# A graph layer over sorted edges: one scheduling context, a longer tail of single steps, and early VectorE operations with one SBUF input

## The chip, the core and the metric

The kernel runs on one NeuronCore of a Trainium2 chip. The core has TensorE (matrix products into PSUM; in profiles PE, its weight loads PEld), VectorE (DVE), ScalarE (ACT), GpSimd (POOL) and SyncE (SP), which run their own instruction queues in order and wait for each other through semaphores. Data come from HBM by DMAs, which SP, ACT and POOL issue. The metric is the device time of one execution in microseconds, as the median of several runs.

## The reference

The layer passes messages along 212,500 edges between 12,500 nodes of 64 features, and the edges are sorted by their destination `dst`:

```
h    = relu(concat(x[src], x[dst], edge_attr) @ mW1 + mb1)      # 212500 x 128
agg  = segment_sum(h @ mW2 + mb2, dst, 12500)                   # 12500 x 64
u    = relu(concat(x, agg) @ uW1 + ub1) @ uW2 + ub2
out  = layernorm(x + u)                                         # per node, no scale or shift
```

All is float32: x is 12500 x 64, edge_attr 212500 x 32, mW1 160 x 128, mW2 128 x 64, uW1 128 x 128, uW2 128 x 64.

## The kernel before

**Two programs.** `ordered` (from L96) relies on the order of the edges: the 384 edges of a group must have their destinations in a window of W = 32 nodes. It also counts on the chip whether that holds, and writes the answer to the one-element tensor `flag`. `unordered` (from L524) is a general program for any edge list. `gnn_layer` (L789) runs `ordered` in one scheduling context of the framework (`TileContext`), which ends with semaphore waits and barriers of all engines, then opens a second context. There every engine loads the flag (`values_load`, L796) and branches (`tc.If`, L798): `unordered` runs only if the flag is 0. With these inputs it is skipped.

**Work in groups.** G = 554 groups of 384 edges (3 tiles of 128; the last group has 148 edges) go through three parts. Each group also needs its rows x[src], which POOL fetches with one indirect DMA per tile (`gather`, L132, 1661 in all), up to AHEAD = 16 groups ahead, into a ring of 20 buffers `own.s`. VectorE writes the one-hot of the destinations within the window beside them (`onehot`, L303).

- `turn` (L309): TensorE transposes the three tiles (L315) into PSUM bank 0 of a buffer; ACT copies the result to `own.st` (L323), beside the edge attributes that SP loads (L263), and sums each row of it, which counts the edges per destination.
- `hidden` (L331): TensorE multiplies by the first layer's weights (L336), where the one-hot rows pick the window's part of x @ mW1 + mb1 from `own.wm`; ACT applies relu (L346, or L348 for the last group) into `own.h`.
- `sums` (L356): TensorE turns the counts into a row (L360) and multiplies relu's result by the one-hot (L362), which sums the messages per destination; VectorE adds both to `agg` (L371) and to row 0 of `xc` (L372).

Every four groups `windows` (L285) computes the next four `own.wm` (PE L289, VectorE copies L294), from columns of `xc` which `places` picks (L282). The second layer's weights are applied after the sum.

**Updates.** `plan` cuts the nodes into 25 chunks of 512 (the last has 212) and says after which group a chunk is closed: chunk 23 after group 546, the last one after all groups. `update` (L378) has four stages: `load` (xin, L384), `first` (PE L389 and L390, ACT L392, VectorE L393), `second` (PE L402, VectorE L404 to L409, ACT square root `rstd` L411) and `third` (VectorE L416, L419, output DMA on SP L423). `step_update` runs one stage each time `sums` is emitted.

**The order of the work** is written by hand: within `manual_schedule` every engine gets its instructions in the order in which they are emitted. `step` (L443) puts up to three parts together. Its first matmul waits for all that the parts need, and only the last matmul of the step counts on the semaphore, so whoever follows waits for the whole step. Steps take the two PSUM buffers `own.ps` in turn. The main loop (L488) at group k runs one step of turn k, hidden k-2 and sums k-4. From k = 548 on (SHORT = 6) `go_on(k, k - 1)` first catches up, in steps that pair one hidden with one sums, and then a step holds turn k alone.

**The front.** While the first gathers are issued, VectorE converts the groups' first destinations (`first_f`, L190, in SBUF), computes each edge's place in its window (`dlc`, 128 x 1662, L201 and L202) and counts the valid ones. For the count, L233 multiplies (place - 31) by place, and L234 compares that with 0 and accumulates:

```
    nc.vector.scalar_tensor_tensor(off, dlc, 1.0 - W, dlc, op0=ALU.add, op1=ALU.mult)
    nc.vector.tensor_scalar(off, off, 0.0, 0.0, ALU.is_le, ALU.add, accum_out=valid)
```

Of the kernel before, what the change touches and what calls it, by code (L numbers as in the profile page):

```python
# [19 lines left out]
P = 128  # L20
# [23 lines left out]
NEAR_GROUPS = 24  # L44
SHORT = 6
TIMES = 4
# [49 lines left out]
def ordered(ctx: ExitStack, tc: tile.TileContext, a, own, ok):  # L96
# [91 lines left out]

    first_f = temp.tile([P, G], F32, name="first_f")
    nc.vector.tensor_copy(first_f, first_i)  # L190
# [38 lines left out]


    off = temp.tile([P, G * TG], F32, name="off")
    valid = temp.tile([P, 1], F32, name="valid")
    nc.vector.scalar_tensor_tensor(off, dlc, 1.0 - W, dlc, op0=ALU.add, op1=ALU.mult)  # L233
    nc.vector.tensor_scalar(off, off, 0.0, 0.0, ALU.is_le, ALU.add, accum_out=valid)  # L234
    low = temp.tile([1, G], F32, name="low")
# [9 lines left out]
    vps = ups.tile([H, CH], F32, name="u_ps")  # L245
    nc.tensor.matmul(vps[0:1, 0:1], ones[:, 0:1], valid, start=True, stop=True)
    nv = temp.tile([1, 1], F32, name="nv")
    nc.vector.tensor_tensor(nv, vps[0:1, 0:1], nwrong, ALU.subtract)
    nc.vector.tensor_scalar(ok, nv, float(E), None, ALU.is_equal)

# [188 lines left out]

    users = [[], []]  # L440
    number = 0

    def step(gt=None, gh=None, gs=None):  # L443


        nonlocal number
        ps, used = own.ps[number % 2], users[number % 2]
        parts = [part(g, ps) for part, g in ((turn, gt), (hidden, gh), (sums, gs))
                 if g is not None]
        did = [i for part in parts for i in part[0]]  # L450
        after(did[0], *used, *(i for part in parts for i in part[1]))
        copies = None
        if gs is not None:
            for b in [b for b in xws if (b - 1) * SB <= gs][:1]:
                last, copies = windows(b, ps[:, 2, (TIMES + 1) * W : (TIMES + 1) * W + H])
                after(last, *used)
                did.append(last)
        for i in did[:-1]:
            tc.no_tile_sem_insts.add(i.ins.name)
            tc.add_to_no_dep_group("quiet", i.ins)  # L460
        used = []
        for n, (_, _, follow) in enumerate(parts):
            if gs is not None and n == len(parts) - 1:
                step_update(gs)
            used += follow(did[-1])
        if copies:
            copies()
            used += [wm_by[b * SB + i] for i in range(min(SB, G - b * SB))]
        users[number % 2] = used
        number += 1  # L470

# [5 lines left out]
    made = summed = 0  # L477

    def go_on(hidden_to, sums_to):

        nonlocal made, summed
        while made < hidden_to or summed < sums_to:
            gh = made if made < hidden_to else None
            gs = summed if summed < sums_to else None
            made, summed = made + (gh is not None), summed + (gs is not None)
            step(None, gh, gs)

    for k in range(G):  # L488
        if k < BITS:
            bit(k)  # L490
        if k % SB == 2:
            inputs(k // SB + 2)
        if k % SB == 1:
            places(k // SB + 1)
        onehot(k + 1)
        if k < G - SHORT:
            made, summed = max(0, k - 1), max(0, k - 3)
            step(k, k - 2 if k > 1 else None, k - 4 if k > 3 else None)
        else:
            go_on(k, k - 1)  # L500
            step(k)
        if k + AHEAD < G:
            gather(k + AHEAD)
    go_on(G, G)
    while now or waiting:
# [6 lines left out]
TAIL = E - FULL * R * P  # L512
LOAD = 8
NEAR = 3
# [9 lines left out]
def unordered(ctx: ExitStack, tc: tile.TileContext, a):  # L524
# [73 lines left out]
    with tc.tile_pool(name="nodes", bufs=3) as np_, tc.tile_pool(  # L598
        name="znodes_ps", bufs=2, space=PSUM
    ) as nps:  # L600
        for base, p, n in CHUNKS:
            s = np_.tile([P, R, H], F32, name="za")
            d = np_.tile([P, R, H], F32, name="zb")
            ps = nps.tile([P, R, 2, H], F32, name="zps")
            for k in range(n):
                nc.tensor.matmul(
                    ps[:p, k].rearrange("p s h -> p (s h)"), xT_sb[:, base + k : base + p * n : n],
                    w1ab.rearrange("k s h -> k (s h)"), start=True, stop=True,
                )
            nc.vector.tensor_copy(s[:p, :n], ps[:p, :n, 0, :])  # L610
            nc.scalar.activation(d[:p, :n], ps[:p, :n, 1, :], AF.Copy)
            rows = slice(base, base + p * n)
            nc.sync.dma_start(by_src[rows, :].rearrange("(p n) h -> p n h", p=p), s[:p, :n])
            nc.scalar.dma_start(by_dst[rows, :].rearrange("(p n) h -> p n h", p=p), d[:p, :n])
# [4 lines left out]
    with tc.tile_pool(name="zef", bufs=3) as efp, tc.tile_pool(  # L619
# [31 lines left out]
        def edges(g):  # L651
            m, p = tiles(g)
            t0 = g * R
            row = eps_.tile([P, R, P], F32, name="row")
            same = ep.tile([P, R, P], F32, name="same")
# [25 lines left out]

            hp = eps_.tile([P, R, H], F32, name="hp")
            t = ef_tiles[g // LOAD]
# [9 lines left out]

            sp = eps_.tile([P, R, H], F32, name="sp")
            for j in range(m):
# [20 lines left out]
    with tc.tile_pool(name="zupd", bufs=2) as up, tc.tile_pool(  # L716
        name="zupd_in", bufs=2
    ) as ip, tc.tile_pool(name="zupd_ps", bufs=2, space=PSUM) as ups, tc.tile_pool(
        name="zupd_ps1", bufs=1, space=PSUM
    ) as ups1:  # L720
        for base, p, n in CHUNKS:
# [14 lines left out]

            hT_ps = ups.tile([H, P * R], F32, name="hT_ps")
            cT_ps = ups1.tile([1, P * R], F32, name="cT_ps")
            for k in range(n):
# [7 lines left out]

            ag_ps = ups1.tile([D, P * R], F32, name="ag_ps")
            nc.tensor.matmul(ag_ps[:, :q], w2, hT[:, :q], start=True, stop=False)
# [5 lines left out]
            for k in range(n):  # L755
                nc.vector.tensor_copy(xk[:, k * p : (k + 1) * p],
                                      xT_sb[:D, base + k : base + q : n])
            u_ps = ups.tile([H, P * R], F32, name="zu_ps")
            nc.tensor.matmul(u_ps[:, :q], u1[:, 0, :], xk[:, :q], start=True, stop=False)
# [3 lines left out]

            o_ps = ups.tile([P, R, D], F32, name="o_ps")
            for k in range(n):
# [22 lines left out]

def gnn_layer(nc, a):  # L789
    with nc.sbuf_tensor("flag", [1, 1], I32) as flag:  # L790
        with ExitStack() as ctx:
            own = Own(nc, ctx)
            with tile.TileContext(nc) as tc, tc.manual_schedule():
                ordered(tc, a, own, flag.ap())
        with tile.TileContext(nc) as tc:
            good = nc.values_load(flag.ap()[0:1, 0:1], min_val=0, max_val=1,  # L796
                                  skip_runtime_bounds_check_because="a comparison's result")
            with tc.If(good == 0):  # L798
                with tc.manual_schedule():
                    unordered(tc, a)  # L800

# [33 lines left out]
```

## Time and profile before

| what | value |
|---|---|
| time, median of 3 runs | 2115.33 us (2114.32 to 2117.07) |
| the profiled execution's own time | 2125.18 us |
| its span, first to last instruction | 2123.5 us |
| busy: POOL / PE / PEld / DVE / ACT | 1578.7 / 1419.4 / 1207.0 / 574.6 / 554.4 us |
| gathers on POOL | 1661, 0.95 us each |
| mean granted TensorE clock | 0.931 |
| HBM read / written | 90.58 MB / 3.20 MB |

The profiled execution is 0.5% above the median of the runs. A line of the timeline has the start in us, the length in us, the engine, the source line, the operation, what it writes and reads, the number of merged instructions, and in brackets the idle time before it and what ended that. A "q" behind an engine's name is its instruction queue. A waits line says which operation waited for which, then the total in us, how many times, and the longest. A line of stretches has, for each engine, its busy time and its instruction count in brackets, then the granted TensorE clock as a share of full speed.

### The profile page before, as it was taken

The page shows a single profiled execution, that of the slowest core. Times are in us where ns is not written, and L with a number is a line of the kernel's source. Part 1 is how long each engine was busy: PE and PEld are TensorE (multiplying, and loading weights), DVE is VectorE, ACT ScalarE, POOL GpSimd, SP SyncE. Part 2 cuts the span into 40 slices and gives each one's busy share as a digit, 9 for nine tenths or more (in the row PEclk, how much of TensorE's full clock was granted, in tenths as well). Part 3 has the DMA queues.
Part 4 walks back from the last instruction along what each step waited for, and adds up shares of the span by engine and source line. Part 5 has one row for each costly group of instructions (what it writes and reads, how often), then busy time and mean ns, then how long its engine had stood idle before and what let it go on. Part 6 is the DMA issues. An engine that isn't in the chain of part 4 may idle for free. (4 is left out here: it accounts for less than half of the span.)

```text
span 2123.5 us, 30687 instructions
## 1 busy us (share of the span) xinstructions
PE 1419.4 (67%) x9439; PEld 1207.0 (57%) x9439; DVE 574.6 (27%) x3190; ACT 554.4 (26%) x1715; POOL 1578.7 (74%) x1668
## 2 busy tenths in 40 slices
PE   2766676676766667667666667676665766666766
PEld 2655565565555556556555556555554655555654
DVE  5222322223222222222223222222222222222222
ACT  1322222222222222222222222222222222222221
POOL 7777777777777777777777777777777777777772
PEclk9999989989999999999999898999999899999996
DMA  4321121122221212121212121221211121212110
GB/s 108 83 47 41 44 43 42 43 44 44 44 44 41 47 38 47 40 44 43 44 41 47 38 47 40 45 47 40 45 43 42 43 44 41 47 40 45 43 42 15
DMA packets 73364, 96.05 MB, mean 45 GB/s; under 512 B 33451, under 2 KB 40842, under 8 KB 73194
## 3 DMA queue, kind: packets, MB, share of 16 engines
q0 software_dynamic: 53152, 54.51, 13.5%
q1 hardware_dynamic: 19128, 39.03, 6.6%
q8 instruction: 80, 1.31, 0.3%
q14 instruction: 90, 0.74, 0.1%
q10 hardware_dynamic: 914, 0.46, 0.1%
HBM read 90.58 MB, written 3.20 MB: 44 GB/s over the span
## 5 line engine op out<-in xcount | busy, mean ns | idle before, releaser
L132 POOL DMA_INDIRECT own_s<-in_x,src_sb x1661 | 1577.9, 950 | 507.5 <-issue 354.3
L315 PE MATMUL own_ps<-own_ident,own_s 128*96 128x128 f32 x1661 | 300.5, 293 | 649.1 <-DVE own_s L303 233.2
L323 ACT ACTIVATE own_st<-own_ps 96x384 f32<-96x384 f32 x554 | 269.2, 486 | 1433.8 <-PE own_ps L362 1029.0
L315 PEld LDWEIGHTS own_ps<-own_ident,own_s 128*96 128x96 f32 x1661 | 172.8, 135 | 746.7 <-ACT own_h L346 671.7
L362 PE MATMUL own_ps<-own_s,own_h 128*128 128x128 f32 x3322 | 569.7, 313 | 0.0
L336 PE MATMUL own_ps<-own_wm,own_st 128*128 128x128 f32 x3322 | 502.1, 291 | 6.1 <-ACT own_st L323 5.4
L371 DVE TENSOR_TENSOR agg<-own_ps,agg 128x32 f32 x554 | 106.5, 192 | 1411.3 <-ACT own_h L346 1388.2
L362 PEld LDWEIGHTS own_ps<-own_s,own_h 128*128 128x128 f32 x3322 | 456.5, 208 | 24.2 <-issue 0.2
L336 PEld LDWEIGHTS own_ps<-own_wm,own_st 128*128 128x128 f32 x3322 | 454.8, 207 | 8.5 <-ACT own_st L323 7.7
L346 ACT ACTIVATE own_h<-own_ps 128x384 f32<-128x384 f32 x553 | 262.8, 475 | 17.6 <-issue 12.9
L294 DVE COPY own_wm<-own_ps 32x128 f32<-32x128 f32 x550 | 155.1, 282 | 6.2 <-issue 0.4
L303 DVE TENSOR_TENSOR own_s<-iota,dlc 128x96 f32<-128x96 f32 x554 | 133.2, 241 | 5.2 <-issue 1.1
L323 ACT ACTIVATION_READ_ACCUMULATOR own_st<-own_ps 96x1 f32 x554 | 105.4, 190 | 0.0
L360 PE MATMUL own_ps<-own_ident,own_counts 32*1 32x32 f32 x554 | 103.8, 187 | 1.1 <-ACT own_h L348 0.6
L372 DVE TENSOR_TENSOR xc<-own_ps,xc 1x32 f32 x554 | 99.2, 179 | 14.1 <-PE u_ps L390 13.5
L360 PEld LDWEIGHTS own_ps<-own_ident,own_counts 32*1 32x1 f32 x554 | 41.1, 74 | 74.1 <-issue 14.1
L282 DVE COPY xw<-xc 66x32 f32 x554 | 61.8, 173 | 2.9 <-DMA xc<-in_xT 2.3
L289 PE MATMUL own_ps<-w1b,xw 66*128 66x128 f32 (+1 forms) x276 | 56.8, 289 | 0.0
L402 PE MATMUL u_ps<-u,u 128*128 128x64 f32 (+1 forms) x196 | 48.5, 391 | 0.5 <-ACT u L392 0.5
L402 PEld LDWEIGHTS u_ps<-u,u 128*128 128x128 f32 (+1 forms) x196 | 47.5, 326 | 1.3 <-ACT u L392 1.1
L289 PEld LDWEIGHTS own_ps<-w1b,xw 66*128 66x128 f32 (+1 forms) x276 | 45.5, 207 | 0.1
L404 DVE TENSOR_TENSOR y<-u_ps,xin 128x256 f32<-128x256 f32 (+1 forms) x25 | 10.5, 419 | 81.9 <-PE u_ps L402 81.9
(57 smaller groups left out, 209.0 us busy)
## 6 DMA issues: line engine op xcount, KB each, us to landing
own_s<-in_x,src_sb POOLq DMA_INDIRECT x1661, 2.4
own_st<-in_efT SPq DMA_DIRECT2D x138, 192.0 KB, 2.8
xin<-in_x SPq DMA_DIRECT2D x24, 128.0 KB, 2.7
out<-o SPq DMA_DIRECT2D x24, 128.0 KB, 2.4
xc<-in_xT SPq DMA_DIRECT2D x12, 179.2 KB, 4.1
dlc_i<-in_dst_cols SPq DMA_DIRECT2D x1, 831.0 KB
xc<-in_xT SPq DMA_DIRECT2D x4, 179.5 KB, 4.3
src_sb<-in_src SPq DMA_DIRECT2D x13, 50.5 KB, 3.6
```

Of the source, the lines that this page charges most:

```text
L132: nc.gpsimd.indirect_dma_start(out=s[:p, j, W:], out_offset=None, in_=x[:, :], in_offset=bass.IndirectOffsetOnAxis(ap=src_sb[:p, g * TG + ...
L289: did = nc.tensor.matmul(wp[: n * W, :], xw[:, :n, :], w1b, start=True, stop=True)
L294: c = nc.vector.tensor_copy(wm[g % NW][:W, :], wp[i * W : (i + 1) * W, :])
L303: places_by[g] = nc.vector.tensor_tensor(own.s[g % RING][:, :, :W], iota.unsqueeze(1).to_broadcast([P, TG, W]), dlc[:, g * TG : (g + 1) * ...
L315: nc.tensor.transpose(xt[:, j * P : j * P + p], s[:p, j, :], ident[:p, :p])
L323: nc.scalar.activation(t[: D + W, c : c + n], xt[:, :n], AF.Copy, accum_out=counts[:, g : g + 1]), step)
L336: nc.tensor.matmul(pre[:p, j, :], t[:, c + j * P : c + j * P + p], wm[g % NW], start=True, stop=True)
L346: relu_by[g] = [nc.scalar.activation(h, pre, AF.Relu)]
L360: did = [nc.tensor.transpose(sg[0:1, TIMES, :], counts[:W, g : g + 1], ident[:W, :W])]
L362: did.append(nc.tensor.matmul(sg[:, :TIMES, :], h[:p, j, :], s[:p, j, :W].unsqueeze(1).to_broadcast([p, TIMES, W]), start=j == 0, stop=j = ...
L371: after(nc.vector.tensor_tensor(agg[:, at], sg[:, 0, :], agg[:, at], ALU.add), step),
L372: after(nc.vector.tensor_tensor(xc[0:1, at], sg[0:1, TIMES, :], xc[0:1, at], ALU.add), step),
```

## The change

- `gnn_layer` opens one context. The flag is a tile of that context, and the load and the branch follow `ordered` in it. The buffers of `Own` now stay allocated beside `unordered`, so that program gets fewer PSUM buffers, shared tags and LOAD = 4; it is still skipped.
- SHORT is 10. From k = 544 on every part is a step of its own with its own count on the semaphore: turn k, then up to two sums, then up to two hidden. `go_on` is gone; after the loop the remaining sums follow.
- `step` takes a list of (part, group). A part uses PSUM buffer g % 2 of its group, and the users of a buffer are kept per part.
- `first_f` lies in the PSUM buffer `own.ps[0]` instead of SBUF. The count of valid places is two comparisons, place >= 0 and place <= 31, each with one input and an accumulator; two matmuls add the two counts, and the constant they are compared with grows by the number of all places.

```
-SHORT = 6
+SHORT = 10
...
-    first_f = temp.tile([P, G], F32, name="first_f")
+    first_f = own.ps[0].rearrange("p a b -> p (a b)")[:, :G]
     nc.vector.tensor_copy(first_f, first_i)
...
     off = temp.tile([P, G * TG], F32, name="off")
-    valid = temp.tile([P, 1], F32, name="valid")
-    nc.vector.scalar_tensor_tensor(off, dlc, 1.0 - W, dlc, op0=ALU.add, op1=ALU.mult)
-    nc.vector.tensor_scalar(off, off, 0.0, 0.0, ALU.is_le, ALU.add, accum_out=valid)
+    valid = temp.tile([P, 2], F32, name="valid")
+    nc.vector.tensor_scalar(off, dlc, 0.0, 0.0, ALU.is_ge, ALU.add, accum_out=valid[:, 0:1])
+    nc.vector.tensor_scalar(off, dlc, W - 1.0, 0.0, ALU.is_le, ALU.add, accum_out=valid[:, 1:2])
...
-    nc.tensor.matmul(vps[0:1, 0:1], ones[:, 0:1], valid, start=True, stop=True)
+    for i in range(2):
+        nc.tensor.matmul(vps[0:1, 0:1], ones[:, 0:1], valid[:, i : i + 1], start=i == 0,
+                         stop=i == 1)
...
-    nc.vector.tensor_scalar(ok, nv, float(E), None, ALU.is_equal)
+    nc.vector.tensor_scalar(ok, nv, float(E + P * G * TG), None, ALU.is_equal)
...
-    users = [[], []]
-    number = 0
-    def step(gt=None, gh=None, gs=None):
-        nonlocal number
-        ps, used = own.ps[number % 2], users[number % 2]
-        parts = [part(g, ps) for part, g in ((turn, gt), (hidden, gh), (sums, gs))
-                 if g is not None]
-        did = [i for part in parts for i in part[0]]
-        after(did[0], *used, *(i for part in parts for i in part[1]))
+    users = {part: [[], []] for part in (turn, hidden, sums)}
+    def step(*work):
+        parts, used = [], []
+        for part, g in work:
+            ps, old = own.ps[g % 2], users[part][g % 2]
+            parts.append((part, g, *part(g, ps)))
+            used += old
+        did = [i for p in parts for i in p[2]]
+        after(did[0], *used, *(i for p in parts for i in p[3]))
         copies = None
-        if gs is not None:
-            for b in [b for b in xws if (b - 1) * SB <= gs][:1]:
-                last, copies = windows(b, ps[:, 2, (TIMES + 1) * W : (TIMES + 1) * W + H])
-                after(last, *used)
-                did.append(last)
+        for part, g, *_ in parts:
+            if part is sums:
+                for b in [b for b in xws if (b - 1) * SB <= g][:1]:
+                    last, copies = windows(b, own.ps[g % 2][:, 2, (TIMES + 1) * W :][:, :H])
+                    did.append(last)
         for i in did[:-1]:
             tc.no_tile_sem_insts.add(i.ins.name)
             tc.add_to_no_dep_group("quiet", i.ins)
-        used = []
-        for n, (_, _, follow) in enumerate(parts):
-            if gs is not None and n == len(parts) - 1:
-                step_update(gs)
-            used += follow(did[-1])
-        if copies:
-            copies()
-            used += [wm_by[b * SB + i] for i in range(min(SB, G - b * SB))]
-        users[number % 2] = used
-        number += 1
+        for part, g, _, _, follow in parts:
+            if part is sums:
+                step_update(g)
+            users[part][g % 2] = follow(did[-1])
+            if part is sums and copies:
+                copies()
+                users[part][g % 2] += [wm_by[b * SB + i] for i in range(min(SB, G - b * SB))]
...
-    def go_on(hidden_to, sums_to):
-        nonlocal made, summed
-        while made < hidden_to or summed < sums_to:
-            gh = made if made < hidden_to else None
-            gs = summed if summed < sums_to else None
-            made, summed = made + (gh is not None), summed + (gs is not None)
-            step(None, gh, gs)
 
     for k in range(G):
         if k < BITS:
...
             places(k // SB + 1)
         onehot(k + 1)
         if k < G - SHORT:
+            step((turn, k), *([(hidden, k - 2)] if k > 1 else []),
+                 *([(sums, k - 4)] if k > 3 else []))
             made, summed = max(0, k - 1), max(0, k - 3)
-            step(k, k - 2 if k > 1 else None, k - 4 if k > 3 else None)
         else:
-            go_on(k, k - 1)
-            step(k)
+            step((turn, k))
+            for _ in range(2):
+                if summed < made:
+                    step((sums, summed))
+                    summed += 1
+            for _ in range(2):
+                if made <= k:
+                    step((hidden, made))
+                    made += 1
         if k + AHEAD < G:
             gather(k + AHEAD)
-    go_on(G, G)
+    while summed < G:
+        step((sums, summed))
+        summed += 1
     while now or waiting:
...
-def gnn_layer(nc, a):
-    with nc.sbuf_tensor("flag", [1, 1], I32) as flag:
-        with ExitStack() as ctx:
-            own = Own(nc, ctx)
-            with tile.TileContext(nc) as tc, tc.manual_schedule():
-                ordered(tc, a, own, flag.ap())
-        with tile.TileContext(nc) as tc:
-            good = nc.values_load(flag.ap()[0:1, 0:1], min_val=0, max_val=1,
-                                  skip_runtime_bounds_check_because="a comparison's result")
-            with tc.If(good == 0):
-                with tc.manual_schedule():
-                    unordered(tc, a)
+@with_exitstack
+def gnn_layer(ctx: ExitStack, nc, a):
+    own = Own(nc, ctx)
+    tc = ctx.enter_context(tile.TileContext(nc))
+    flag = ctx.enter_context(tc.tile_pool(name="flag", bufs=1))
+    ok = flag.tile([1, 1], I32, name="ok")
+    with tc.manual_schedule():
+        ordered(tc, a, own, ok)
+    good = nc.values_load(ok[0:1, 0:1], min_val=0, max_val=1,
+                          skip_runtime_bounds_check_because="a comparison's result")
+    with tc.If(good == 0):
+        with tc.manual_schedule():
+            unordered(tc, a)
```

More of the change, by code (lines that the diff above doesn't have):

```diff
@@ L512 @@
 TAIL = E - FULL * R * P
-LOAD = 8
+LOAD = 4
 NEAR = 3
@@ L598, in unordered @@
     with tc.tile_pool(name="nodes", bufs=3) as np_, tc.tile_pool(
-        name="znodes_ps", bufs=2, space=PSUM
+        name="znodes_ps", bufs=1, space=PSUM
     ) as nps:
@@ L653, in edges @@
             t0 = g * R
-            row = eps_.tile([P, R, P], F32, name="row")
+            row = eps_.tile([P, R, P], F32, name="row", tag="zps")
             same = ep.tile([P, R, P], F32, name="same")
@@ L680, in edges @@
             nc.vector.tensor_tensor(rows_to[:p, :m], go[:p, :m], dst_f[:p, t0 : t0 + m], ALU.add)
-            hp = eps_.tile([P, R, H], F32, name="hp")
+            hp = eps_.tile([P, R, H], F32, name="hp", tag="zps")
             t = ef_tiles[g // LOAD]
@@ L692, in edges @@
             nc.scalar.activation(h[:p, :m], pre[:p, :m], AF.Relu)
-            sp = eps_.tile([P, R, H], F32, name="sp")
+            sp = eps_.tile([P, R, H], F32, name="sp", tag="zps")
             for j in range(m):
@@ L717, in unordered @@
         name="zupd_in", bufs=2
-    ) as ip, tc.tile_pool(name="zupd_ps", bufs=2, space=PSUM) as ups, tc.tile_pool(
-        name="zupd_ps1", bufs=1, space=PSUM
-    ) as ups1:
+    ) as ip, tc.tile_pool(name="zupd_ps", bufs=2, space=PSUM) as ups:
         for base, p, n in CHUNKS:
@@ L735, in unordered @@
             nc.vector.tensor_tensor(tab[:p, 0, :n], tab[:p, 0, :n], tab[:p, 2, :n], ALU.add)
-            hT_ps = ups.tile([H, P * R], F32, name="hT_ps")
-            cT_ps = ups1.tile([1, P * R], F32, name="cT_ps")
+            hT_ps = ups.tile([H, P * R], F32, name="hT_ps", tag="zps")
+            cT_ps = ups.tile([1, P * R], F32, name="cT_ps", tag="zps")
             for k in range(n):
@@ L746, in unordered @@
             nc.vector.tensor_copy(cT[:, :q], cT_ps[:, :q])
-            ag_ps = ups1.tile([D, P * R], F32, name="ag_ps")
+            ag_ps = ups.tile([D, P * R], F32, name="ag_ps", tag="zps")
             nc.tensor.matmul(ag_ps[:, :q], w2, hT[:, :q], start=True, stop=False)
@@ L757, in unordered @@
                                       xT_sb[:D, base + k : base + q : n])
-            u_ps = ups.tile([H, P * R], F32, name="zu_ps")
+            u_ps = ups.tile([H, P * R], F32, name="zu_ps", tag="zps")
             nc.tensor.matmul(u_ps[:, :q], u1[:, 0, :], xk[:, :q], start=True, stop=False)
@@ L762, in unordered @@
             nc.scalar.activation(u[:, :q], u_ps[:, :q], AF.Relu, bias=u1b)
-            o_ps = ups.tile([P, R, D], F32, name="o_ps")
+            o_ps = ups.tile([P, R, D], F32, name="o_ps", tag="zps")
             for k in range(n):
```

## The prediction

> **What bounds the kernel now.** I read the groups of the page first. POOL runs nothing but gathers, and each is 0.95 us of work and about 0.30 us of issue:
>
> ```profile
> L132 POOL DMA_INDIRECT own_s<-in_x,src_sb x1661 | 1577.9, 950 | 507.5 <-issue 354.3
> L315 PE MATMUL own_ps<-own_ident,own_s 128*96 128x128 f32 x1661 | 300.5, 293 | 649.1 <-DVE own_s L303 233.2
> ```
>
> From start to start the median is 1.251 us and the mean 1.2549, so 1660 steps take 2083.1 us: the first gather starts at 2.97 and the last at 2086.09. Its idle time is put down to issue, in pieces of 0.3 us, so nothing holds the chain up once it runs. TensorE follows it: in the steady state group g's transposes (L315) start a median 2.63 us after the start of the group's last gather, which is the landing. So the time is 2.97 of front, the gather chain, and 37 us behind its last link. A change can gain at the front, where the chain is held up, or behind the end; TensorE's, ACT's and DVE's work between lies under the chain.
>
> Next I read the timeline of the front, for gathers longer than 0.95:
>
> ```profile
> 10.53 1.89 DVE L202 TENSOR_TENSOR dlc<-dlc,first_f 128x1662 f32<-128x1662 f32 x1
> 10.91 2.32 POOL L132 DMA_INDIRECT own_s<-in_x,src_sb  x1 [0.30 <-issue]
> ...
> 14.77 1.87 DVE L233 SCALAR_TENSOR_TENSOR off<-dlc 128x1662 f32<-128x1662 f32 x1
> 14.79 2.67 POOL L132 DMA_INDIRECT own_s<-in_x,src_sb  x1 [0.30 <-issue]
> ...
> 16.67 1.88 DVE L234 TENSOR_SCALAR_CACHE_REDUCE off<-off 128x1662 f32<-128x1662 f32 x1
> 17.77 0.95 POOL L132 DMA_INDIRECT own_s<-in_x,src_sb  x1 [0.31 <-issue]
> ...
> 20.00 0.72 DVE L243 TENSOR_TENSOR wrong<-first_f,high 1x554 f32<-1x554 f32 x1
> 20.27 1.27 POOL L132 DMA_INDIRECT own_s<-in_x,src_sb  x1 [0.30 <-issue]
> ```
>
> A gather that starts under L202 or L233 (VectorE operations with both inputs in SBUF) ends about 0.81 us after that operation ends: 2.32 and 2.67 us in place of 0.95. Under L234, with one input and an accumulator, it takes 0.95. Under L243 (two SBUF inputs, one partition) it takes 1.27.
>
> Then the timeline of the end. The PE lines are the transposes of groups 547, 548, 549 and 553; the POOL line is the last gather:
>
> ```profile
> 2067.44 0.84 PE L315 MATMUL own_ps<-own_ident,own_s 128*96 128x128 f32 x3 [0.98 <-ACT own_h L346]
> ...
> 2076.63 0.49 PE L315 MATMUL own_ps<-own_ident,own_s 128*96 128x128 f32 x3
> ...
> 2081.27 0.49 PE L315 MATMUL own_ps<-own_ident,own_s 128*96 128x128 f32 x3
> ...
> 2086.09 0.90 POOL L132 DMA_INDIRECT own_s<-in_x,src_sb  x1 [0.30 <-issue]
> ...
> 2102.25 0.62 PE L315 MATMUL own_ps<-own_ident,own_s 128*96 128x128 f32 x2
> ```
>
> Group 547 starts 2.61 us after its last gather starts, group 548 8.05 us, 549 8.93, and 553 16.17. So the data have long been there, and TensorE's own order sets the end. Three steps of old work (groups 546 and 547) run ahead of 548's transposes. After that each group costs hidden(k-1), sums(k-2), transposes(k) and the ACT copy in a line; from 2092.92 on that repeats every 4.67 us, against 3.75 us per three gathers. The clock has part in it (stretches: length, busy PE, PEld, DVE, ACT, POOL, granted clock, DMA, GB/s):
>
> ```profile
> 1000.00:1500.00 500.00, 342.75 (x2276) 292.09 (x2274) 129.88 (x744) 133.01 (x413) 378.32 (x399) 0.93 0.20 44
> 2072.00:2089.00 17.00, 13.19 (x81) 10.24 (x80) 5.61 (x31) 4.05 (x11) 11.33 (x13) 1.00 0.14 25
> 2089.00:2103.00 14.00, 11.74 (x47) 9.54 (x47) 2.74 (x15) 3.27 (x11) 0.00 (x0) 0.51 0.04 13
> ```
>
> Last I read SyncE's waits, for what lies behind the last VectorE operation (it ends at 2112.57 + 0.54 = 2113.11):
>
> ```profile
> SPq L798 <- SPq L798: 3.9, 1, 3.9
> ...
> SPq L793 <- DMA out<-o: 1.9, 1, 1.9
> ```
>
> SyncE waits 1.9 us for the last output to land at the end of the first context (L793). After the branch (L798) it stands 3.9 us until its next instruction, and the records of the other engines show the same: TensorE's branch itself takes 3.40 us, VectorE goes from 2117.21 to 2121.46. Of the 10.36 us from 2113.11 to 2123.47, 2.5 are issue and landing, 1.15 context end, 0.5 the flag's load, 4 the branch, and the rest semaphores and the second context's end.
>
> **The change, part by part.** The sum is against the profiled execution: 2125.18 us, span 2123.5. That is 9.85 above the median of 2115.33; I can't place that difference. 5.9 ns on each gather would make it, and the steps below would then be the same, so I take the gain off the median.
>
> **Front.** First_f moves to PSUM, so L202 and L242/L243 read one SBUF input; L233 becomes a second accumulating comparison like L234. Start to start, the gathers held up took 2.629, 2.975 and 1.572 us; against 1.251 that is 1.38 + 1.72 + 0.32 = **3.42 us** which go. The gather at 9.42 (+0.24) lies under the cast L201, which stays. Here a rule speaks against the change. The Trainium skill, page "SBUF — State Buffer", section "Who interferes with whom", says that single-source operations such as tensor_scalar can run in a two-port mode and then lock GpSimd out, though not the form that also writes an accumulator. The new comparisons are of the excepted form. The nearest row, L234, takes 1.88 us for 1662 elements and leaves the gather at 0.95. By the row they cost nothing. Were they of the locking form, each would hold one gather up to its own length less the 0.14 us that a gather ran before the lock; with L201's 1.03 us that is 0.9 each, and the front's gain is 1.6. I take the row. No row shows a cast into PSUM, or L202 with a PSUM input: at the least they cost what they do now (0.55, 1.89), at the most I allow 0.3 us each, the size of the PSUM copy L226 (0.29). That, and 0.08 for a second accumulator read and some 0.2 for one more [1,1] matmul, would only make VectorE late for the agg memset, the xw copies at 35.48 and TensorE's first transposes at 38.29. There TensorE is nine groups behind and has caught up by group 20 (lag 32.6 us at group 0, 2.65 at 20): hidden. Without that cover it would be under 1 us. The ring of 20 groups leaves room too: group 20's gathers, near 78 us, need group 0's transposes of 38 us.
>
> **Main loop.** In step k the three parts used PSUM buffer k%2 and do so still, with the same waits; SP's and POOL's queues keep their order. Nothing.
>
> **Tail.** From k = 544: transposes k; up to two sums; up to two hidden. Each signals its own end, so ACT copies group k while TensorE does sums. Warm costs, from rows at 2059.86 to 2062.0: transposes 0.35, hidden 0.83, sums 1.0 with the count row. Groups 544 and 545 each carry two sums and two hidden: 0.35 + 2.0 + 1.7 = about 4 us against 3.75. 546 carries 3.2, 547 2.2: caught up. Chunk 23's update opens at group 546. Its first part (L389, L390: 2.04 us, 2079.54 to 2081.43) goes behind sums 547, its second (L402: 2.08) behind sums 548, with windows (0.4). In the second, y and the statistics (about 2.0, 2087.00 to 2088.88) come ahead of rstd on ACT, and relu 549 is queued behind rstd, and sums 549 and hidden 550 wait for it. With group 548 starting at 0: 549 starts at 4.2 (data at 3.75), 550 at 9.1 (7.5), 551 at 13.0 (11.25), 552 at 15.4 (15.0). Group 553 is free at 17.8 and its data come at 18.75. At full clock nothing of the slip is left.
>
> The clock is the unknown. The same skill, page "TensorE: Matmul & The Clock Gate", section "HAM oscillation — how this bites in real kernels", asks only that no TensorE gap exceed about 3.4 us. By that the new tail (gaps near 1.5 us) stays warm and slips 0. The trace differs: in the steady state, whose longest wait for a gather is 2.4 us,
>
> ```profile
> PE own_ps L315 <- DMA own_s<-in_x,src_sb: 183.5, 121, 2.4
> ```
>
> the clock still is 0.93, that is, half speed for 14% of the time, in windows of 3.4 or 6.8 us. One such window costs up to 1.7 or 3.4 us where it strikes, with 0.95 us and some 1.5 us per later group to take it up. I take 0.8 us, between 0 and 3.5.
>
> So group 553 starts at 2086.09 - 3.42 + 2.6 + 0.8 = 2086.1, where it was 2102.25: 16.2 us earlier, of which 3.4 is the front and 12.8 the tail. Behind it, from 553's start to the add's end was 5.29 (2102.25 to 2107.54). Now the copy (0.5) lies under sums 552 and relu 553 no longer waits for them: 0.45 transposes + 1.05 sums + 0.79 hidden + 0.5 relu + 0.05 + 1.4 sums + 0.25 add = 4.5, so **0.8** less. The last update (5.57 us to 2113.11) stays.
>
> **One context.** The end of the first context goes, and with it the wait for the landing ahead of the branch. Each engine loads the flag and branches behind its own last work. SyncE issues the output (0.3 us), loads (0.5), branches (4.0), and the landing at +2.5 lies under that. With 0.6 of semaphores and 1.45 of context end it is 6.9 us behind the last VectorE operation in place of 10.36: **3.5**. The other bound: the block waits at its entry for everything before, the landing too; then only the context's end (1.1) is saved. No row shows a branch in a context with work ahead of it. Nearest is L798, which has no wait between load and branch, so I take 3.5.
>
> **Sum:** 16.2 + 0.8 + 3.5 = 20.5 us; 2115.33 - 20.5 = **2095**. The profiled execution would be near 2104.7, its span near 2103.
>
> **Rivals.** (a) *The tail was shorter outside the profile, or the new one is hit by the clock.* For it: 4.67 us per group needs the clock at 0.51; warm, the old line is 3.2 us (0.35 transposes, 0.75 copy, 0.83, 1.05, 0.2), so it would gain 0.5 per group on the gathers, and the lag at 553 be some 6 instead of 13.6. Against: 2089 to 2103 was cold throughout, and I know no reason for a better clock unprofiled. The gain falls by 5 to 9: about 2103. (b) *The branch waits for the landing:* 2.4 of the 3.5 stay, about 2097.5. (c) *Slower:* one context for all could give each gather a wait more at its issue. Each 12.3 ns on 1661 gathers is 20.5 us, and beyond that the sign turns; 25 ns, about one semaphore record on POOL (0.02), gives 2095 + 41 = 2136. Against: ring and waits of the gathers are the same lines. (d) *It does not do what it says:* the parts still wait for one another in the tail through ACT's order, and the branch gains nothing; the front's 3.4 alone is 2112.
>
> **How the numbers follow.** Likeliest case 0.58, own range 2092 to 2099; (a) 0.20; (b) 0.12; (c) 0.04; (d) 0.06. Low end: no slip (0.8), a warm end chain (about 1.2) and the runs' own 1.4 give 2091.5. (a) is taken in to 2104; (c), (d) and a tenth are left out. 0.2% (4.2 us) is about what a measurement of this kernel can tell from no change. (d) at -3.4 with its spread is half within: same 0.03. Slower: (c) 0.04. Faster: 0.93.
>
> **What would show it.** Right: no gather above 1.3 us between 10 and 21 us; the last gather starting near 2082.7; lag of the transposes under 4 us at 553; SyncE's wait for the landing gone; about 6.9 us behind the last VectorE operation. Wrong: a median step of the gathers above 1.251; lags over 6 at groups 549 to 553; a wait for the output ahead of the branch; rstd holding ACT for more than the 2 us above.

## The result and the profile after

The changed kernel takes 2103.22 us (median of 6 runs, 2102.39 to 2104.61). Beside it on the same chip the kernel before takes 2117.2 us (6 runs, 2114.32 to 2118.85). The ratio is 0.9936, 95% interval 0.9923 to 0.9949: 14.0 us faster. The forecast was 2095, with a range of 2091 to 2104.

The profiled execution of the changed kernel is one of these runs, with 2103.22 us and a span of 2101.4. That of the kernel before had 2125.18 us and a span of 2123.5, which is 8 us above its median. So the two profiles lie 22.1 us apart where the medians lie 14.0 apart, and the difference between them must not be read as the gain.

The front after, from the timeline:

```profile
9.32 1.53 POOL L132 DMA_INDIRECT own_s<-in_x,src_sb  x1 [0.30 <-issue]
...
9.73 1.01 DVE L201 CAST dlc<-dlc_i 128x1662 f32<-128x1662 int32 x1
...
10.77 1.89 DVE L202 TENSOR_TENSOR dlc<-dlc,own_ps 128x1662 f32<-128x1662 f32 x1
11.16 0.94 POOL L132 DMA_INDIRECT own_s<-in_x,src_sb  x1 [0.30 <-issue]
...
12.97 1.86 DVE L234 TENSOR_SCALAR_CACHE_REDUCE off<-dlc 128x1662 f32<-128x1662 f32 x1
13.66 0.94 POOL L132 DMA_INDIRECT own_s<-in_x,src_sb  x1 [0.30 <-issue]
...
14.88 1.88 DVE L235 TENSOR_SCALAR_CACHE_REDUCE off<-dlc 128x1662 f32<-128x1662 f32 x1
...
14.91 0.94 POOL L132 DMA_INDIRECT own_s<-in_x,src_sb  x1 [0.30 <-issue]
```

The gathers under L202 and the two accumulating comparisons take 0.94 us, where 2.32 and 2.67 stood. The one that starts just ahead of the cast L201 takes 1.53; before, 1.19. In 11 of the study's 14 profiles a gather starts ahead of the cast, by up to 0.54 us, and ends 0.12 us behind the cast's end.

The tail after, from the same view. The PE lines are the transposes of group 544, the count row of sums 540, the transposes of 545, the count row of sums 544, hidden 546, and the transposes of 550 and 553; the POOL line is the last gather:

```profile
2049.04 0.50 PE L318 MATMUL own_ps<-own_ident,own_s 128*96 128x128 f32 x3 [1.52 <-DVE own_s L306]
...
2050.21 0.18 PE L363 MATMUL own_ps<-own_ident,own_counts 32*1 32x32 f32 x1 [0.67 <-ACT own_st L326]
...
2056.09 0.53 PE L318 MATMUL own_ps<-own_ident,own_s 128*96 128x128 f32 x3 [0.63 <-ACT own_h L349]
...
2061.08 0.19 PE L363 MATMUL own_ps<-own_ident,own_counts 32*1 32x32 f32 x1 [0.67 <-ACT own_st L326]
...
2063.92 0.94 PE L339 MATMUL own_ps<-own_wm,own_st 128*128 128x128 f32 x6 [0.59 <-DVE own_wm L297]
...
2078.16 0.88 PE L318 MATMUL own_ps<-own_ident,own_s 128*96 128x128 f32 x3 [1.37 <-DVE own_wm L297]
...
2078.95 0.90 POOL L132 DMA_INDIRECT own_s<-in_x,src_sb  x1 [0.30 <-issue]
...
2086.53 0.42 PE L318 MATMUL own_ps<-own_ident,own_s 128*96 128x128 f32 x2
```

Group 553 starts 7.58 us after the last gather's start, against 16.17 before and 2.6 in the steady state. The lag grows at two places: 2.54 at group 544, 5.85 at 545; 5.90 at 549, 9.19 at 550. Between them it is not made good (5.90 at 546, 6.96 at 547, 5.56 at 548). The brackets from sums 540 to the transposes of 550 show waits that the prediction did not have.

The granted clock in the tail (columns as before: length, busy PE, PEld, DVE, ACT, POOL, clock, DMA share, GB/s):

```profile
2051.10:2054.50 3.40, 3.40 (x16) 2.97 (x15) 2.00 (x11) 0.00 (x0) 2.49 (x4) 0.50 0.14 25
...
2075.00:2082.00 7.00, 5.63 (x26) 4.91 (x26) 4.29 (x22) 1.25 (x4) 3.72 (x4) 0.52 0.17 41
2082.00:2092.00 10.00, 7.93 (x54) 6.01 (x52) 1.64 (x10) 3.21 (x12) 0.00 (x0) 1.00 0.02 5
```

And the end, SyncE's wait across the branch (now L799):

```profile
SPq L799 <- SPq L799: 2.6, 1, 2.6
```

SyncE's waits no longer have one for the output's landing, and from the last VectorE operation (2095.05 + 0.54 = 2095.59) to the end at 2101.41 it is 5.82 us, where it was 10.36.

The two profiles side by side, the sum of all places:

| place | before | after | gain | predicted |
|---|---|---|---|---|
| first gather's start | 2.97 | 2.89 | 0.1 | 0 |
| gathers held up among the first 16, over the median step | 3.87 | 0.77 | 3.1 | 3.4 |
| 1660 steps at the median (1.251, 1.249) | 2076.66 | 2073.34 | 3.3 | 0 |
| held up later | 2.59 | 1.95 | 0.6 | 0 |
| lag of group 553 | 16.17 | 7.58 | 8.6 | 12.8 |
| its start to the add of agg | 5.28 | 4.27 | 1.0 | 0.8 |
| last update, to the last VectorE operation | 5.58 | 4.79 | 0.8 | 0 |
| from there to the end | 10.36 | 5.82 | 4.5 | 3.5 |
| sum | | | 22.1 | 20.5 |

### The profile page after: what moved, and what is told of

Its sections match the earlier page's. It is cut to its first block, busy times and chain, and to the rows that moved or that the text cites. A ratio compares the mean times of both kernels' runs of the same rounds, so it can differ in the third digit from the quotient of the medians.

```text
span 2101.4 us, 30666 instructions
## 1 busy us (share of the span) xinstructions
PE 1412.9 (67%) x9441; PEld 1202.9 (57%) x9441; DVE 575.0 (27%) x3191; ACT 553.4 (26%) x1715; POOL 1571.9 (75%) x1668
## 4 chain that ended last, share of the span: by engine, by line
PE 40%; DMA 22%; issue 14%; POOL 12%; ACT 6%; DVE 5%; SPq 0%; POOLq 0%; ACTq 0%; DVEq 0%
DMA own_s<-in_x,src_sb 21%; PE own_ps L365 15%; POOL own_s L132 12%; PE own_ps L339 12%; PE own_ps L318 8%; ACT own_h L349 4%; ACT own_st L326 2%; PE own_ps L363 2%; DVE xc L375 1%; DVE own_s L306 1%; PE own_ps L292 1%; PE u_ps L405 1%; DVE agg L374 1%; PE u_ps L392 1%; PE u_ps L393 1%
## 5 line engine op out<-in xcount | busy, mean ns | idle before, releaser
L363 PEld LDWEIGHTS own_ps<-own_ident,own_counts 32*1 32x1 f32 x554 | 41.1, 74 | 78.0 <-issue 13.6
L407 DVE TENSOR_TENSOR y<-u_ps,xin 128x256 f32<-128x256 f32 (+1 forms) x25 | 10.5, 419 | 78.2 <-PE u_ps L405 78.2
```

What stands on the lines that cost most here:

```text
L363: did = [nc.tensor.transpose(sg[0:1, TIMES, :], counts[:W, g : g + 1], ident[:W, :W])]
```

## The experiments

The theory: front about 3 us, end about 4.5, and the tail the rest of the 14, because the tail of the kernel before is usually shorter than in its profile. The rival: the tail is worth the 13.6 of the prediction, and something else took back 6 us. The trace after speaks against the rival already: even against the long tail of the profile before, the lag of 553 with its last group and update gains 8.6 + 1.0 + 0.8 = 10.4 us.

One thing has to be known for the numbers: the five series ran on different chips. On one the kernel before took 2118.63 us, as first measured. On the four others the same program took 2506 to 2534 us. Ratios are within a series and taken round by round, so that they can differ in the fourth place from the quotient of the two medians.

**The kernel before, again** (no edit).

> The kernel before, unchanged, profiled again. If the profiled execution of 2125.2 us was an unusual one (a tail at half clock), its profile now shows a span near 2115, a lag of group 553's transposes of 6 to 10 us in place of 16.2, and a TensorE clock above 0.51 behind the last gather. If the profile itself costs time, the span is near 2123 again with the same lag. Ratio 1.000 within 0.002.

Measured: 2534.71 us beside 2533.66 (ratio 1.000, 0.9991 to 1.0009). The gathers' group and POOL's longest waits in its profile:

```profile
L132 POOL DMA_INDIRECT own_s<-in_x,src_sb x1661 | 1577.2, 950 | 872.1 <-issue 431.1
```

```profile
POOL own_s L132 <- remote: 290.3, 129, 10.8
```

One gather costs the same 0.95, but POOL stands idle 872 us in place of 507, in waits of up to 10.8 us which the first profile of this kernel does not have. Its last gather and ACT's copy of group 553:

```profile
2449.97 0.90 POOL L132 DMA_INDIRECT own_s<-in_x,src_sb  x1 [0.30 <-issue]
```

```profile
2512.42 0.28 ACT L323 ACTIVATE own_st<-own_ps 96x148 f32<-96x148 f32 x1
```

62 us lie between; the data of some 16 groups are there, and the ring of buffers holds the gathers back. On this chip TensorE sets the pace (granted clock 0.781). The lag of group 553 therefore says nothing on the old tail here; how long the work from group 547 on takes does, and is compared below.

**The front alone.**

```
-    first_f = temp.tile([P, G], F32, name="first_f")
+    first_f = own.ps[0].rearrange("p a b -> p (a b)")[:, :G]
...
-    nc.vector.scalar_tensor_tensor(off, dlc, 1.0 - W, dlc, op0=ALU.add, op1=ALU.mult)
-    nc.vector.tensor_scalar(off, off, 0.0, 0.0, ALU.is_le, ALU.add, accum_out=valid)
+    nc.vector.tensor_scalar(off, dlc, 0.0, 0.0, ALU.is_ge, ALU.add, accum_out=valid[:, 0:1])
+    nc.vector.tensor_scalar(off, dlc, W - 1.0, 0.0, ALU.is_le, ALU.add, accum_out=valid[:, 1:2])
```

> The early VectorE operations alone, all else as before. The prediction's step says 3.4 us faster (gathers under L202, L233 and L243 at 0.95 us), about 2113.5 against 2117. If the whole shortfall of the forecast lay here, nothing is gained: gathers of 2 us and more would be seen elsewhere. A lengthened gather under a cast at 9.3 us would take 0.3 back.

Measured: 2531.72 beside 2533.66, ratio 0.9995 (0.9986 to 1.0004): no difference. Its timeline shows the hold-ups gone:

```profile
9.24 1.68 POOL L132 DMA_INDIRECT own_s<-in_x,src_sb  x1 [0.30 <-issue]
...
11.22 0.94 POOL L132 DMA_INDIRECT own_s<-in_x,src_sb  x1 [0.31 <-issue]
...
14.97 0.94 POOL L132 DMA_INDIRECT own_s<-in_x,src_sb  x1 [0.30 <-issue]
```

Over the first 15 steps, the very first left out, 0.7 us are held up, against 3.0 and 3.5 in the two profiles of the kernel before on such chips. The same kernel in another series:

> The early VectorE operations alone again, now where the gathers set the pace. The prediction's step says 3.4 us faster (about 2114 against 2117.5), less 0.3 for a cast at 9.3 us: 3.1. If the gathers' head start is lost before the end: 0. Its profile shows another old tail: lag of group 553 between 8 and 17 us.

2505.56 beside 2506.45, ratio 1.0004 (0.9995 to 1.0013), 0.4 us held up. So the mechanism is there on both chips, and it is worth nothing where the gathers run into their ring anyway.

**The tail alone** (SHORT = 10, the new `step` and the new loop, in two contexts with the old front):

```
-SHORT = 6
+SHORT = 10
...
-            go_on(k, k - 1)
-            step(k)
+            step((turn, k))
+            for _ in range(2):
+                if summed < made:
+                    step((sums, summed))
+                    summed += 1
...
```

> SHORT = 10 and single steps alone, two contexts and the old front. The prediction's step says 13.6 us faster (2103.5). The rival, that the tail before was shorter than its profile showed, says 5 to 8 us (2109 to 2112), with the lag of group 553 near 7 us, as in the changed kernel's profile (7.58).

> The tail alone again, on a chip where the kernel before takes about 2117 us: in the first series it took 2533 us, with TensorE standing still some 160 times, so that TensorE and not the gathers set the pace. The prediction's step says 13.6 us faster here (about 2103.5), the rival of a shorter tail before says 5 to 8 (2109 to 2112). If TensorE sets the pace again (about 2533), 2 us faster.

Measured: 2531.62 beside 2533.66, ratio 0.9989 (0.9980 to 0.9998), and 2528.41 beside 2530.92, ratio 0.9991 (0.9982 to 1.0000): 2 to 2.5 us, the second at the edge of no difference. The expectation for a TensorE that sets the pace holds; which size the tail has at the gathers' pace these two cannot say. With the second went one more profile of the kernel before:

> The kernel before, profiled again on the same chip as the tail alone. If the profiled execution of 2125.2 us had an unusually slow tail, group 553's transposes lag 6 to 12 us here in place of 16.2, and the span is near 2115.

2530.58 beside 2530.92 (1.0004, 0.9991 to 1.0016), again at TensorE's pace.

**One context alone** (`gnn_layer` of the changed kernel, with the smaller PSUM shares of `unordered`):

```
...
-        with tile.TileContext(nc) as tc:
-            good = nc.values_load(flag.ap()[0:1, 0:1], min_val=0, max_val=1,
...
+    good = nc.values_load(ok[0:1, 0:1], min_val=0, max_val=1,
...
```

> One scheduling context alone, old front and old tail. The prediction's step says 3.5 us faster (6.9 us behind the last VectorE operation), the changed kernel's profile says 4.5 (5.82). If the branch waits for the landing: 1.1. If a wait is added to each gather: slower, with a median step above 1.251 us.

Measured: 2529.53 beside 2533.66, ratio 0.9983 (0.9974 to 0.9992), that is 4.3 us, in agreement with the trace's 4.5. SyncE's waits, ahead of it the kernel before in the same series:

```profile
SPq L798 <- SPq L798: 4.2, 1, 4.2
SPq L793 <- DMA out<-o: 1.9, 1, 1.9
```

```profile
SPq L797 <- SPq L797: 2.5, 1, 2.5
```

From the last VectorE operation to the end it is 5.76 us here. In all profiles of the study it is 10.2 to 10.5 us with two contexts and 5.75 to 5.97 with one. The median step of the gathers is 1.249: no wait was added.

**The changed kernel again, and more single steps.** These three ran together on the chip at the gathers' pace. In the second, SHORT = 20; in the third SHORT = G, so that no group goes through the paired loop:

```
-SHORT = 10
+SHORT = 20
```

> The changed kernel, unchanged, beside the kernel before. Where the gathers set the pace (before about 2117 us): 14 us faster, as measured first. Where TensorE sets it, as in the two series before (2531 and 2534 us): the front's 3.4 us is hidden under TensorE and the tail cannot catch up with data that are long there, so only the end's 4.5 us and some 2 to 3 of the tail are left: 6 to 8 us faster. If the three parts add up whatever sets the pace: 20.

> The changed kernel with single steps for the last 20 groups in place of 10. Theory: in the changed kernel's profile the two groups with double work put TensorE 3.3 us behind the gathers, and the update of chunk 23 adds as much; ten groups more take up the first. Where the gathers set the pace: 2 to 3 us faster than the changed kernel, lag of group 553 under 6 us. Where TensorE sets it: the same within 2 us.

> The changed kernel with single steps from the first group on, so that sums k-1 and hidden k follow transposes k throughout, with three counted steps per group in place of one. Where the gathers set the pace: as with 20 groups. Where TensorE sets it, 554 groups show what a counted step costs TensorE: at 50 ns for each of two more per group it is 55 us slower; if single steps keep ACT and VectorE better ahead, faster.

| kernel | median us | ratio to before (2118.63) | lag of 549 | 553 | span of its profile |
|---|---|---|---|---|---|
| changed (10) | 2103.68 | 0.9935 (0.9920 to 0.9950) | 5.16 | 7.23 | 2102.6 |
| 20 | 2100.90 | 0.9923 (0.9907 to 0.9939) | 2.74 | 4.29 | 2100.0 |
| all | 2098.04 | 0.9908 (0.9890 to 0.9926) | 4.68 | 6.73 | 2098.8 |

The changed kernel repeats its 14 to 15 us. With 20 groups the lag at 553 is 2.9 us less and the time 2.8 us less: the catching up of groups 544 and 545 does cost what its profile shows. The transposes of the groups 550, 551, 552 and 553 there, with the last gather:

```profile
2076.69 0.88 PE L318 MATMUL own_ps<-own_ident,own_s 128*96 128x128 f32 x3 [1.37 <-DVE own_wm L297]
...
2080.35 0.56 PE L318 MATMUL own_ps<-own_ident,own_s 128*96 128x128 f32 x3
2080.83 0.90 POOL L132 DMA_INDIRECT own_s<-in_x,src_sb  x1 [0.30 <-issue]
...
2082.76 0.50 PE L318 MATMUL own_ps<-own_ident,own_s 128*96 128x128 f32 x3
...
2085.12 0.42 PE L318 MATMUL own_ps<-own_ident,own_s 128*96 128x128 f32 x2
```

Even from a lag of 2.74 at group 549 the update takes it to 5.85 at 550, with the same wait of 1.37 us for the window copies. From 551 on a group takes 2.4 us, so 1.3 is made good from 551 to 552; group 553 has two gathers only, and there it is 0.1. With all groups single the main loop costs TensorE nothing at the gathers' pace. That kernel is the fastest of all, yet not by its tail: its lag at 553 is 6.73. In its profile the last gather starts at 2077.43 against 2080.83, 3.4 us earlier: 1.7 is a median step of 1.249 in place of 1.250, and 2.4 are fewer later hold-ups (0.1 in place of 2.5 us, counted as in the table above), less 0.7 at the front. How much of the 2.9 us between the last two medians is lasting stays open. Both lie under the changed kernel in all their runs (its least is 2103.33, the most of these is 2102.57).

**The changed kernel with the old tail** (SHORT = 6, the old `step` and `go_on`):

```
-SHORT = 10
+SHORT = 6
...
+            go_on(k, k - 1)
+            step(k)
...
```

> The changed kernel with the old tail (SHORT = 6, paired catch-up steps and go_on), so the front and the one context are kept. Where the gathers set the pace and before is about 2117 us: the prediction's steps (front 3.4, context 3.5) say 2110, and the tail would be worth the rest to 2103.5; the traces' sizes (front 3.1, context 4.5) say 2109.5 and a tail of 6. If the tail were worth the 13.6 of the prediction, this kernel would stand at 2117. Its profile shows a second old tail: a lag of group 553 near 10 us says that the 16.2 of the first profile was unusual, 16 that it is the rule.

> The changed kernel with the old tail once more, for a chip where the kernel before takes about 2117 us. The prediction's steps (front 3.4, context 3.5) say 2110, the traces' sizes (front 3.1, context 4.5) 2109.5, and the tail is worth the rest, 6 us. If the tail is worth the 13.6 of the prediction: 2117. Lag of group 553's transposes near 10 us if the first profile's 16.2 was unusual. Where TensorE sets the pace (before about 2500 to 2530 us): 2 to 4 us faster than before, and the size of the tail stays open.

Both fell on chips where TensorE sets the pace: 2503.97 beside 2506.45, ratio 0.9989 (0.9980 to 0.9999), and 2527.05 beside 2533.04, ratio 0.9976 (0.9965 to 0.9987), 2.5 and 6.0 us from front and context together. So no second profile has the old tail at the gathers' pace.

**The old tail in eight profiles.** The old tail is nevertheless in seven more profiles, those of the two repeats, the two of the front alone, the context alone and the two above. From the transposes of group 547 on the data are there in all eight (in the first profile the lag is 8 us and more from 548 on), so its length from there is set by the order of the work itself and not by the gathers, and can be compared. The stretch from the transposes of 547 to those of 553 in the first profile, and below it with the context alone (columns as before):

```profile
2067.44:2102.25 34.81, 28.87 (x145) 23.89 (x146) 8.83 (x47) 7.56 (x22) 14.98 (x16) 0.75 0.10 21
2481.26:2510.57 29.31, 23.28 (x147) 18.89 (x146) 8.83 (x47) 8.38 (x24) 0.00 (x0) 0.94 0.02 7
```

From the transposes of 547 to the end of the last VectorE operation, with the part of it at half clock:

| profile | us | at half clock |
|---|---|---|
| before, the first | 45.7 | 25.2 |
| old tail | 43.7 | 21.2 |
| front alone | 43.7 | 20.9 |
| before, again | 41.2 | 13.6 |
| front alone, second | 40.5 | 11.7 |
| context alone | 39.7 | 8.9 |
| before, again, second | 38.8 | 7.9 |
| old tail, second | 38.6 | 4.7 |

The first profile has the longest of the eight tails and the most half clock. A straight line (36.5 us, and 0.35 more for each us at half clock) meets all eight within 0.5 us. The seven others are 2.0 to 7.0 us shorter, 5.2 in the median.

## Why the prediction was right or wrong

The time lies in the stated range, but not by the working that was held likeliest: that case, 2092 to 2099, was missed, and the range went up to 2104 only for rival (a), which had a chance of 0.20. A sign that the prediction named for being wrong came true as well: lags over 6 at groups 549 to 553, with 9.19 at 550 and 7.58 at 553 where under 4 was expected. Between the two profiles, leaving aside the gathers' steps, later hold-ups and start, the 20.5 us came out as 18.0: 0.3 less at the front, 4.2 less in the lag of 553, 1.0 more at the end, 0.2 and 0.8 more for the last group and the last update. The other 4.0 down to the measured 14.0 are the base.

**Front: right in mechanism, a little too large.** 3.1 of 3.42 us in the two profiles. The rest is the cast L201: the gather now starts 0.4 us ahead of it in place of 0.04, and is held until the cast's end. The rule weighed there was settled by the row: two accumulating comparisons leave the gathers under them at 0.94. The rest of the front did stay hidden: groups' lags are 2.6 us in the steady state before and after.

**One context: right, too small by 1.** The landing lies under the load and the branch, as the step said. The term that was mis-sized is the branch: 4.0 was taken, and SyncE stands 2.6. That one is shown by the context alone too. Rival (b), a branch that waits for the landing, and rival (c), a wait at each gather, are out: SyncE's wait for the output is gone, and the median step is 1.249 to 1.250 us.

**Tail: right in direction; the slip was mis-sized.** "I take 0.8 us, between 0 and 3.5" is the step that failed. Measured against the lag of 2.6: 5.0 us in the first profile of the changed kernel and 4.6 in the second. The working's claim that groups 546 and 547 catch up did not come true: 546 was worked out at 3.2 us and took 4.8. Two terms of it:

- Waits that the working lacked: 0.67 for the copy of group 544 ahead of sums 540, 0.63 for relu 543 ahead of transposes 545, 1.37 for the window copies ahead of transposes 550, 2.7 us together. Two more keep group 546 from catching up: 0.67 for the copy of group 546 ahead of sums 544, and 0.59 for the window copies ahead of hidden 546. With the windows' own products (0.39), which the working left out there, they make 546's 4.8. None of the five is in the part's own list of needs and users. Each is on a reader of the same PSUM buffer, `own.ps[g % 2]`, in another bank. That points at a wait for the whole buffer; it is argued from five places, and separate buffers for the parts were not tried.
- The clock. Half clock from 2051.1 to 2054.5 and from 2075.0 to 2081.8 in the first of these profiles lies on just the two places where TensorE has the most to do. The second profile has only the later window, and 0.7 us less lag at 545. By the rule that the prediction weighed (the Trainium skill, page "TensorE: Matmul & The Clock Gate", section "HAM oscillation — how this bites in real kernels") no such window would have been: TensorE's longest stand between 2030 and 2082 us is 1.57 us.

Group 549 to 550 was worked out at 4.9 us; it took 7.0: the wait of 1.37, and hidden 549 at half clock with 1.59 in place of 0.83. From 551 to 553 the steps of 2.4 us are as worked out. One reading in the working is wrong: group 553 has two gathers, so its data come at 17.5 and not at 18.75, and 0.3 of slip is left even at full clock. The term for group 553's own chain (0.8) measured 1.0. The last update's 0.8 was not in the sum; all of it is the clock, since its two products into u_ps up to ACT's relu took 1.82 us at half clock before and 1.02 at full clock after.

**The base: "I take the gain off the median".** The prediction said that it could not place the 9.85 us between the profiled execution and the median, and let the steps stand as if it lay on the gathers. It did only in part. The median step of that execution was 1.251, of the changed kernel 1.249 and 1.250: at most 3.3 us. Of 14.0 us between the medians, front and end take 3.1 + 4.5, so for the tail with its last group and update there remain **6.4**, where 13.6 were forecast and 10.4 lie between the profiles. If front and end gain in every run what they gain between the profiles, and the gathers' steps are otherwise alike, the old tail is usually some 4 us shorter than in the profile. This is the first half of rival (a), which said about 2103; its second half, the new tail hit by the clock, is part of the slip above, and the waits on the PSUM buffers were in neither. The eight profiles bear the shorter tail out: the first one's is the longest, the others are 5.2 us shorter in the median, and the difference goes with the time at half clock. The runs agree: the kernel before varies by 9 us beside the repeated changed kernel (2112.53 to 2121.64), the changed kernel by 1 (2103.33 to 2104.28). What stays open is how long the old tail is in the usual run at the gathers' pace, since the seven others come from chips where TensorE sets the pace, and why the first profile of the kernel before got so much half clock.

## What to carry to other kernels

Before a tail is priced from one profile, set that execution against the median of the runs: where it lies above, the tail may be the part that is out of the ordinary, and the gain there has to be cut by that much. Here one and the same tail took 38.6 to 45.7 us, by its time at half clock. At the end of a pipeline let each part of a group signal for itself and start with it early enough that the extra work of the switch is made good before the last group: here 20 groups in place of 10 gave 2.8 us. Price a single step of a buffer by all its readers, not only by those that the step lists, until a run with separate buffers shows that the others cost nothing.

## What the runs showed of the hardware

**A chip can change what bounds a kernel.** The same program took 2118 us on one chip and 2506 to 2534 on four others. Gathers cost 0.95 us on each; on the slow ones the granted clock is 0.78 to 0.80 in place of 0.93, and TensorE falls more than 60 us behind the gathers. It is not the clock alone: after the first 100 us TensorE stands still for more than 1.8 us 182 times in the profile of the kernel before there, 701 us together, against 32 times and 64 us in the first profile of that kernel. What holds it there stays open. There a gain in the gathers is worth nothing (1.0004), and one at the end its full 4.3 us.

**What still holds gathers up.** In the changed kernel 10 of the 25 additions of the bias to xin (L396, both inputs in SBUF) fall on a gather and cost 1.8 us in sum; in the profile with 20 groups it is 14 and 2.8. One of them:

```profile
293.64 0.40 DVE L396 TENSOR_TENSOR xin<-xin,u2b 128x256 f32<-128x256 f32 x1
293.68 1.19 POOL L132 DMA_INDIRECT own_s<-in_x,src_sb  x1 [0.30 <-issue]
```

The Trainium skill, page "SBUF — State Buffer", section "Who interferes with whom", says that a VectorE operation with two SBUF inputs contends with a GpSimd instruction that reads SBUF; the trace agrees here as at the front. By the row of L202 above, which has one input in PSUM, u2b in PSUM should take this away; it was not tried.
